# Layer 3's step reordered: maxima and copies before subtraction and exponential, counting at the end of a slot, other MLP turns, and an earlier last channel mixing

## The chip, the core and the metric

The kernel runs on one core of one Trainium2 chip. The metric is the device time of one launch in microseconds; all times below are microseconds unless they are marked ns. The core has five engines with queues of their own, each worked off in order: PE (TensorE, matrix products and transposes; its weight loads are listed as PEld), DVE (VectorE), ACT (ScalarE), POOL (GpSimd) and SP (SyncE, which here only issues DMAs). POOL issues DMAs too.

## The reference

Four layers over a batch of 4 with 512 positions and 512 channels, all in float32. Layer 0 is a cross attention with a layer norm, layers 1 and 2 are recurrent (a time mixing with a scan, then a channel mixing), and layer 3, which most of the change is in, is an attention of x over the concatenation of the context and x itself, followed by an MLP:

```python
# layers 1 and 2, the channel mixing at the end of each
xc = _ln(x, ln2_w, ln2_b)
sxc = jnp.concatenate([state[:, i0][:, None], xc[:, :-1]], axis=1) - xc
xk2 = xc + sxc * fmaa_k
xr2 = xc + sxc * fmaa_r
rr = jax.nn.sigmoid(xr2 @ fWr.T)
kk = jnp.square(jax.nn.relu(xk2 @ fWk.T))
x = x + rr * (kk @ fWv.T)
...
# layer 3: x is the context, latents are the result of layer 2
h = jnp.concatenate([x, latents], axis=1)
q = (latents @ q_w + q_b).reshape(b, k_len, NH, DH)
kv = (h @ kv_w + kv_b).reshape(b, p + k_len, NH, DH, 2)
attn = jnp.einsum('bkhd,bnhd->bhkn', q, kmat) / DH
attn = jnp.where(full_mask[:, None, None, :], attn, -jnp.inf)
attn = jax.nn.softmax(attn.astype(jnp.float32), axis=-1).astype(q.dtype)
attn_out = jnp.einsum('bhkn,bnhd->bkhd', attn, v).reshape(b, k_len, H)
attn_out = attn_out @ out_w + out_b + residual
out = rmsnorm(attn_out, postnorm_w)
out = jax.nn.gelu(out @ mlp_w1 + mlp_b1) @ mlp_w2 + mlp_b2
return out + residual
```

In layer 3 there are 16 heads of 32 channels, 512 queries and 1024 keys for each of the 4 batch entries; the mask covers the first 512 keys.

## The kernel before

The order of the instructions on PE, DVE, ACT and POOL is the order of the Python code (a manual schedule); a framework adds the semaphores and places SP's DMAs.

**The recurrent layers** work on 16 units, each of one layer, one batch entry and 256 positions. A unit takes eight scan steps g; after the last one (g = 128) the stages that follow the scan run on for some twenty steps more. `mixes`, `outputs` and `channels` are generators: each `yield g, phase` names the step, counted from the unit's first, and the place in it (EARLY, SOON, MID, LATE) where it goes on. `outputs` (steps 9 to 15) normalises the scan's result and adds it to x; for the last unit it ends at step 135. Its two powers on POOL (`gn_rs`, L932 and L934) are followed by ACT copies into `rp` and a broadcast `pbc` by PE. `channels` (steps 19 to 27) is the channel mixing: layer norm (`stats`, `scaled` into z), transposes on PE into xc (`turned`, ptn), the shifted difference sxc on POOL (`shift`), the mixtures xk and xr (`shifted`: four scalings on ACT, then `added`, an accumulating DMA that POOL issues, L583), and three products with the weights fk, fr and fv (PE tiles pm, pr, pv, all recorded under the helper line L72), of which the last is combined on DVE (L1034) and added to x by another accumulating DMA. Counted from the first unit, the last unit's channel mixing runs from step 139 to 147, the one before it from 131 to 139.

From step 129 on each step also takes one piece of layer 3's beginning (`beside`): two pieces of `begin(0)`, which transposes x of batch 0 (ptx, L1144) and adds the output bias to it on POOL (L1149), and five each of `prep(0, 0)` and `prep(0, 1)` (products pq, two pk, two pv for a group of four heads). These twelve pieces end at step 140.

**Layer 3** works through 32 units (b, m, h): batch entry, group of four heads, half of the queries (256). A unit has four steps of 256 keys, so 128 steps in all; a group (b, m) has eight, counted as c = 0 to 7 below, and a step is called a slot. The work of step i, by helper:

- `scores(i)`: 16 matmuls into the two PSUM tiles ps (L1199); they exist once, so the next step's scores need them read out.
- `kept(i, 1)` and `kept(i, 0)`: two ACT copies of ps to w in SBUF (L1213).
- `largest(i)`: four DVE instructions that keep a running maximum (L1230, L1232, L1234), with the mask for the first 512 keys.
- At a unit's end, in the first step of the next one: `gathered` transposes the maxima (ptm, L1243) and reduces them on DVE (L1244); `spread` transposes the result back (pb, L1254) and ACT copies it to mb (L1259).
- `lowered(i - 4)`: one DVE subtraction of mb from w (L1266); `weights(i - 4)`: the exponential on ACT (L1281, L1284).
- `values(i - 5)`: the products with v into po (L1305). po is one tile for both halves of the queries. In batch 0 the count of the weights (pn, by a product with ones) is accumulated by the same helper; in the other batches POOL adds the weights up (`added`, acc, L1295 and L1299), each time released by `ticked`, a tiny DVE memset and POOL copy that put it behind the subtraction (L1271, L1272), and `counted` makes pn from acc.
- `divided(unit)`: reciprocal of pn (L1332) and product with po into y (L1335).
- Turns: at the steps named in `turns` a piece of `prep` for the next group, and at those in `ready` a piece of `finish(b - 1)`, the output product (pout), the norm (its transposes ptn, L1351), and the MLP in eight blocks `hidden` (ph, Gelu L1378) and `closed` (po under L72, added to x in L1388). Each turn of `hidden` or `closed` is 32 or 16 full matmuls.

The order within a step, before: scores, one copy, counting, values (in the second step of a unit, i % 4 = 1, values come last), subtraction, the sums, exponential, maxima, the other copy, division, turns. In the first step of a unit, where mb is made, maxima and the second copy stand ahead of the subtraction. `finish` has 19 turns: two with two pout each, one with only the scaling and the transposes ptn, and two for each of eight blocks. The loop ran five slots past the last step, with the remaining turns; the last batch's `finish` came then.

## Time and profile before

| quantity | value |
|---|---|
| three runs, median | 3744.62 (3740.18 to 3747.02) |
| the profiled execution | 3743.32, span 3741.6 |
| PE busy | 3452.7, 92% of the span |
| DVE, ACT, POOL busy | 2722.9, 1904.6, 1742.6 |
| mean granted PE clock | 0.958 |
| last scan step's product (py) | at 2255.5 |
| first maxima of layer 3 (L1234) | at 2405.7 |
| groups of batch 0, start to start | 59.5, 58.9, 60.1 (the last: 64.0, first group of batch 1) |
| batches 1 to 3, from 2689.5 to the last unit's ptm | 879.1 |
| from there to the last batch's first pout | 39.4 |
| the last batch's `finish` | 133.6 |

The page tells how long each engine was busy; it cuts the span into 40 slices of some 94, lists the chain of work that ended last, and groups instructions by line with their mean length and the idle time of their engine before them. A time line of one engine gives start, length, line, operation, what it wrote and read, and in brackets the idle time before it and who ended it. A clock of 0.5 means that PE's clock was granted half of the time, and its matmuls then take about twice as long.

### The profile page before, as it was taken

The page shows a single profiled execution, that of the slowest core. Times are in us where ns is not written, and L with a number is a line of the kernel's source. Part 1 is how long each engine was busy: PE and PEld are TensorE (multiplying, and loading weights), DVE is VectorE, ACT ScalarE, POOL GpSimd, SP SyncE. Part 2 cuts the span into 40 slices and gives each one's busy share as a digit, 9 for nine tenths or more (in the row PEclk, how much of TensorE's full clock was granted, in tenths as well). Part 3 has the DMA queues.
Part 4 walks back from the last instruction along what each step waited for, and adds up shares of the span by engine and source line. Part 5 has one row for each costly group of instructions (what it writes and reads, how often), then busy time and mean ns, then how long its engine had stood idle before and what let it go on. Part 6 is the DMA issues. An engine that isn't in the chain of part 4 may idle for free. (4 is left out here: it accounts for less than half of the span.)

```text
span 3741.6 us, 55701 instructions
## 1 busy us (share of the span) xinstructions
PE 3452.7 (92%) x22400; PEld 1973.3 (53%) x22400; DVE 2722.9 (73%) x3883; ACT 1904.6 (51%) x2862; POOL 1742.6 (47%) x1040
## 2 busy tenths in 40 slices
PE   8999999998899999999999978788899999989889
PEld 3333333365566666666656634445556556555556
DVE  6777777679988888888888891287766666666631
ACT  4776776534444444444444432266555555655531
POOL 4777777524444444444444443000265555565540
PEclk9999999898999999999999988899999999999999
DMA  4000000056677777777777766100022212212124
GB/s 153 24 12 23 12 9 20 24 138 136 143 174 180 181 190 176 174 179 178 181 171 178 177 152 165 44 12 24 18 70 97 74 45 94 68 60 74 64 95 135
DMA packets 188241, 385.83 MB, mean 103 GB/s; under 512 B 18064, under 2 KB 44816, under 8 KB 185936
## 3 DMA queue, kind: packets, MB, share of 16 engines
q1 hardware_dynamic: 149680, 250.67, 20.8%
q0 software_dynamic: 38304, 131.61, 19.3%
q8 instruction: 177, 2.90, 0.3%
q14 instruction: 80, 0.66, 0.1%
HBM read 246.45 MB, written 4.19 MB: 67 GB/s over the span
## 5 line engine op out<-in xcount | busy, mean ns | idle before, releaser
L291 POOL TENSOR_TENSOR aT<-aT,nmT 128x1536 f32<-128x1536 f32 x124 | 428.8, 3462 | 206.7 <-ACT aT L289 183.4
L253 DVE CUSTOM_DVE_ANT_0 sc<-psc,nm 128x512 f32<-128x512 f32 x512 | 353.7, 691 | 147.6 <-PE psc L241 89.9
L1213 ACT COPY w<-ps 128x1024 f32<-128x1024 f32 x256 | 258.0, 1008 | 315.5 <-PE ps L1199 291.0
L870 DVE TENSOR_TENSOR ry<-kv,o_r 128x1024 f32<-128x1024 f32 x256 | 398.5, 1597 | 7.2 <-PE pm L72 0.5
L1299 POOL TENSOR_TENSOR acc<-acc,w 128x1024 f32<-128x1024 f32 x144 | 364.6, 2532 | 3.9
L1266 DVE TENSOR_TENSOR w<-w,mb 128x2048 f32<-128x2048 f32 x128 | 294.1, 2311 | 6.4 <-ACT mb L1259 6.4
L865 DVE TENSOR_TENSOR_SCAN kv<-W,kv 128x1032 f32<-128x1032 f32 x128 | 295.8, 2311 | 0.0
L289 ACT COPY aT<-pst 128x512 f32<-128x512 f32 x372 | 196.5, 594 | 179.1 <-PE pst L278 178.6
L583 POOL DMA_DIRECT2D kv<-A x127 | 111.8, 880 | 361.6 <-DVE kv L838 227.1
L1272 POOL COPY mark<-tick 128x1 f32<-128x1 f32 x118 | 63.9, 541 | 460.2 <-DVE tick L1271 376.3
L297 ACT ACTIVATE aT<-aT 128x2048 f32<-128x2048 f32 x128 | 246.7, 1929 | 5.4 <-POOL aT L291 4.7
L72 PE MATMUL po<-l_m,hT 128*128 128x512 f32 x512 | 236.1, 616 | 0.0
L72 PE MATMUL ph<-nT,l_m 128*128 128x256 f32 x1024 | 233.1, 386 | 1.4 <-DVE nT L1355 1.4
L1199 PE MATMUL ps<-q,kT 32*128 32x256 f32 x2048 | 163.7, 429 | 62.6 <-ACT w L1213 62.6
L72 PEld LDWEIGHTS ph<-nT,l_m 128*128 128x128 f32 x1024 | 195.8, 193 | 41.9 <-issue 11.6
L1230 DVE TENSOR_TENSOR run<-ps,run 128x512 f32<-128x512 f32 x256 | 170.8, 687 | 62.4 <-PE ps L1199 57.4
L278 PE MATMUL pst<-q,km 32*128 32x512 f32 x1024 | 207.1, 645 | 9.5 <-DVE mxs L253 5.8
L241 PE MATMUL psc<-km,q 32*128 32x512 f32 x1024 | 198.3, 650 | 0.8 <-ACT q L222 0.8
L884 PE MATMUL py<-ry,k 128*32 128x512 f32 x1024 | 162.5, 629 | 37.4 <-DVE ry L870 26.7
L1388 DVE TENSOR_TENSOR x<-po,x 128x512 f32<-128x512 f32 x64 | 44.1, 690 | 183.9 <-PE po L72 183.9
L832 DVE TENSOR_TENSOR kv<-vr,o_k 128x1024 f32<-128x1024 f32 x128 | 155.5, 1215 | 25.3 <-ACT S L856 25.1
L832 DVE TENSOR_TENSOR A<-vr,o_k 128x1024 f32<-128x1024 f32 x128 | 155.3, 1213 | 23.3 <-DMA kv<-A 22.9
(271 smaller groups left out, 7320.2 us busy)
## 6 DMA issues: line engine op xcount, KB each, us to landing
l_m<-in_L_W SPq DMA_DIRECT2D x64, 1024.0 KB, 5.1
kv<-A POOLq DMA_DIRECT2D x127, 516.0 KB, 6.0
L_wk<-in_L_Wk SPq DMA_DIRECT2D x16, 1024.0 KB, 7.9
L_wr<-in_L_Wr SPq DMA_DIRECT2D x16, 1024.0 KB, 7.4
L_wv<-in_L_Wv SPq DMA_DIRECT2D x16, 1024.0 KB, 5.8
L_wg<-in_L_Wg SPq DMA_DIRECT2D x16, 1024.0 KB, 8.0
L_wo<-in_L_Wo SPq DMA_DIRECT2D x64, 256.0 KB, 4.9
L_fk<-in_L_fWk SPq DMA_DIRECT2D x16, 1024.0 KB, 6.6
```

Source lines behind the costliest of these rows:

```text
L72: nc.tensor.matmul(ps, lhsT, rhs, start=(i == 0), stop=(i == len(pairs) - 1))
L241: nc.tensor.matmul(psc, d["q"][g][rs, lt * P : (lt + 1) * P], d["km"][rs, a, :], start=True, stop=True, tile_position=(32 * r, 0),)
L253: nc.vector.tensor_tensor_reduce(sc, ps[r], d["nm"][lt], 1.0, -3.0e38, ALU.add, ALU.max, mxs[:, a, lt, c : c + 1])
L278: nc.tensor.matmul(pst, d["km"][rs, a, s * P : (s + 1) * P], d["q2", a][rs, :], start=True, stop=True, tile_position=(32 * r, 0),)
L291: nc.gpsimd.tensor_tensor(w[:, n:, :], w[:, n:, :], nmT[:, None, :].to_broadcast([P, NR - n, L]), ALU.add)
L297: nc.scalar.activation(w, w, AF.Exp)
L832: nc.vector.tensor_tensor(dst[:, :, 1:], half(vrs[q, e].rearrange("p q f l -> p (q f) l")), half(d["k"][:, i : i + 1, :]).to_broadcast([P, ...
L865: nc.vector.tensor_tensor_scan(flat(kv), flat(W[g % 2]), flat(kv), 0.0, ALU.mult, ALU.add)
L870: nc.vector.tensor_tensor(y, kv[:, 4 * h : 4 * h + 4, None, :TP].to_broadcast([P, 4, 2, TP]), d["r"][:, i].rearrange("p (o m) -> p o m", o ...
L1213: nc.scalar.copy(ws[i][:, 2 * c : 2 * c + 2].rearrange("p r e q -> p (r e q)"), st[b]["ps"][c].rearrange("p r e q -> p (r e q)"),)
L1266: nc.vector.tensor_tensor(w, w, mb, ALU.subtract)
L1299: nc.gpsimd.tensor_tensor(d["acc", m, h], d["acc", m, h], w[:, :, e, :], ALU.add)
```

## The change

In the recurrent layers, the last unit's channel mixing begins three steps sooner, its xk and xr are made on DVE alone, and its last addition to x is done on DVE. Layer 3's bias adds for batch 0 are put behind the whole stage. In layer 3's step the maxima and the second copy now stand ahead of the subtraction in every step; for batches 1 to 3 the counting and the division stand behind the turns, ahead of the delayed values. The last unit's weights are counted by PE, as batch 0's are. `finish` has 18 turns; the one that held only transposes is joined to the turn before it. The turns of `prep` in the first group of batches 1 to 3 move to steps 0, 3, 4, 5 and 6. What ran past the last step is written out by hand.

The diff, without the other `yield`s that get `- sh`:

```diff
+        SHIFT = 3
...
+            ends = q == len(units) - 1
+            sh = SHIFT if ends else 0
             xs = xn[b][hf * NT : (hf + 1) * NT]
             nm, rstd = stats("cx", xs)
-            yield 21, EARLY
+            yield 21 - sh, EARLY
...
             def shifted(name, i):
                 dst = mq.tile([P, KC, TS], F32, tag="cx", name=name, bufs=BUFS["cx"])
                 for k in range(KC):
-                    nc.scalar.activation(dst[:, k], sx[:, k], AF.Copy, scale=vec[:, k, i : i + 1])
-                added(dst, cur)
+                    scale = vec[:, k, i : i + 1]
+                    if ends:
+                        nc.vector.scalar_tensor_tensor(dst[:, k], sx[:, k], scale, cur[:, k], ALU.mult, ALU.add)
+                    else:
+                        nc.scalar.activation(dst[:, k], sx[:, k], AF.Copy, scale=scale)
+                if not ends:
+                    added(dst, cur)
                 return dst
...
-            yield 27, LATE
+            yield 27 - sh, LATE
             for lt in range(NT):
-                added(xs[lt], rr[:, lt])
+                if ends:
+                    nc.vector.tensor_tensor(xs[lt], xs[lt], rr[:, lt], ALU.add)
+                else:
+                    added(xs[lt], rr[:, lt])
...
-            follow(q, (19, LATE), channels(q))
+            follow(q, (19 - (SHIFT if q == len(units) - 1 else 0), LATE), channels(q))
...
                     if k == 1:
                         yield
+                if b:
+                    biased(b)
+                yield
+
+            def biased(b):
                 for x in xn[b]:
                     nc.gpsimd.tensor_tensor(x, x, ob, ALU.add)
-                yield
...
-                if b == 0 and j == 0:
-                    d["pn"] = ps_s.tile([P, HQ], F32, tag="s", name="pn")
+                own = alone((b, m, h))
+                if own and j == 0:
+                    d["pn", m, h] = ps_s.tile([P, HQ], F32, tag="s", name="pn")
                 for e in range(2):
                     ends = dict(start=(j == 0 and e == 0), stop=(j == NS - 1 and e == 1))
                     columns(po[:, h, :], lambda r: v[:, 2 * j + e, 32 * r : 32 * r + 32], lambda r: w[:, r, e, :], **ends)
-                    if b == 0:
-                        columns(d["pn"], lambda r: ones, lambda r: w[:, r, e, :], **ends)
+                    if own:
+                        columns(d["pn", m, h], lambda r: ones, lambda r: w[:, r, e, :], **ends)
...
                 b, m, h = u
                 acc = st[b]["acc", m, h]
-                pn = st[b]["pn"] = ps_s.tile([P, HQ], F32, tag="s", name="pn")
+                pn = st[b]["pn", m, h] = ps_s.tile([P, HQ], F32, tag="s", name="pn")
...
-                    if lt % 2:
+                    if lt == 1:
                         yield
-                scaled(aos[-1], before)
                 normed(0)
                 yield
+                scaled(aos[-1], before)
...
+            def alone(u):
+                return u[0] == 0 or u == units[-1]
...
-                for c in (0, 1, 3, 5, 7) if opens or not nxt else (1, 2, 3, 5, 7) if m else (1, 2, 3, 7):
+                for c in (0, 1, 3, 5, 7) if opens or not nxt else (1, 2, 3, 5, 7) if m else (1, 2, 7):
...
-                for c in (1, 2, 4, 6, 7) if b == 0 else (2, 2, 4, 6, 6) if opens else (0, 0, 4, 6, 6):
+                at = (1, 2, 4, 6, 7) if b == 0 else (2, 2, 4, 6, 6) if opens else (0, 0, 4, 6, 6) if m else (0, 3, 4, 5, 6)
+                for c in at:
                     turns.setdefault(base + c, []).append(gen)
-            ready.update(range(NU, NU + VAL))
...
+            biased(0)
+
+            for i in range(NU):
                 over = None
-                for b0, at in ((True, i - VAL), (False, i - VAL - 1)):
-                    if 0 <= at < NU and at % NS == NS - 1 and (units[at // NS][0] == 0) == b0:
+                for own, at in ((True, i - VAL), (False, i - VAL - 1)):
+                    if at >= 0 and at % NS == NS - 1 and alone(units[at // NS]) == own:
                         over = units[at // NS]
-                last = units[i // NS - 1] if 0 < i <= NU and i % NS == 0 else None
+                last = units[i // NS - 1] if i and i % NS == 0 else None
                 low, val = i - NS, i - VAL
-                val = val if 0 <= val < NU else None
-                sums = added(val) if val is not None and units[val // NS][0] else None
+                sums = added(val) if val >= 0 and not alone(units[val // NS]) else None
                 if last:
                     gathered(last)
-                if i < NU:
-                    scores(i)
-                    kept(i, 1)
-                if over and over[0]:
-                    counted(over)
-                if val is not None and i % NS != 1:
+                scores(i)
+                kept(i, 1)
+                if val >= 0 and i % NS != 1:
                     values(val)
                 if last:
                     spread(last)
-                if sums and last:
-                    ticked()
-                    next(sums)
-                if 0 <= low < NU and not last:
+                largest(i)
+                kept(i, 0)
+                if low >= 0:
                     lowered(low)
                     if sums:
                         ticked()
                         for _ in sums:
                             pass
                     weights(low)
-                elif sums and not last:
-                    for _ in sums:
-                        pass
-                if i < NU:
-                    largest(i)
-                    kept(i, 0)
-                if last:
-                    lowered(low)
-                    if sums:
-                        ticked()
-                        for _ in sums:
-                            pass
-                    weights(low)
-                if over:
+                if over and over[0] == 0:
                     divided(over)
-                    if over[1:] == (KC - 1, 1):
-                        for _ in rest:
-                            pass
-                        rest = finish(over[0])
                 if i in ready:
                     next(rest, None)
                 for gen in turns.get(i, ()):
                     next(gen, None)
-                if val is not None and i % NS == 1:
+                if over and over[0]:
+                    counted(over)
+                    divided(over)
+                if val >= 0 and i % NS == 1:
                     values(val)
+                if over and over[1:] == (KC - 1, 1):
+                    for _ in rest:
+                        pass
+                    rest = finish(over[0])
+
+            gathered(units[-1])
+            values(NU - VAL)
+            spread(units[-1])
+            for j in range(NU - NS, NU):
+                lowered(j)
+                weights(j)
+            ticked()
+            for _ in added(NU - VAL):
+                pass
+            next(rest, None)
+            values(NU - NS)
+            values(NU - NS + 1)
+            next(rest, None)
+            values(NU - NS + 2)
+            counted(units[-2])
+            divided(units[-2])
+            values(NU - 1)
+            divided(units[-1])
             for _ in rest:
+                pass
+            for _ in finish(B - 1):
                 pass
```

`alone` and `biased` are the new functions; the rest of the calls are those described above.

More of the change, by code (lines that the diff above doesn't have):

```diff
@@ L978, in channels @@
             vec, d = small[li]["vec"], st[q]
+            ends = q == len(units) - 1
+            sh = SHIFT if ends else 0
             xs = xn[b][hf * NT : (hf + 1) * NT]
             nm, rstd = stats("cx", xs)
-            yield 21, EARLY
+            yield 21 - sh, EARLY
             z = scaled("cx", xs, nm, rstd)
-            yield 22, EARLY
+            yield 22 - sh, EARLY
             cur = mq.tile([P, KC, TS], F32, tag="xc", name="xc", bufs=1)
@@ L987, in channels @@
             nc.scalar.copy(last, cur[:, :, TS - 1])
-            yield 22, MID
+            yield 22 - sh, MID
             sx = mq.tile([P, KC, TS], F32, tag="sxc", name="sxc", bufs=1)
@@ L994, in shifted @@
                 for k in range(KC):
-                    nc.scalar.activation(dst[:, k], sx[:, k], AF.Copy, scale=vec[:, k, i : i + 1])
-                added(dst, cur)
+                    scale = vec[:, k, i : i + 1]
[5 more added lines that the diff above has]
+                    added(dst, cur)
                 return dst
-            yield 23, EARLY
+            yield 23 - sh, EARLY
             xk = shifted("xk", V_FK)
-            yield 23, LATE
+            yield 23 - sh, LATE
             xr = shifted("xr", V_FR)
-            yield 24, MID
+            yield 24 - sh, MID
             kk = mq.tile([P, KC, TS], F32, tag="cx", name="kk", bufs=BUFS["cx"])
@@ L1012, in channels @@
                 nc.scalar.activation(kk[:, m : m + 2, :], kk[:, m : m + 2, :], AF.Square, scale=0.5**0.5)
-            yield 25, MID
+            yield 25 - sh, MID
             fr = load_w(t[n + "fWr"], n + "fr")
@@ L1023, in channels @@
                 nc.scalar.activation(rr[:, lt], prs[lt], AF.Tanh, scale=0.5)
-            yield 26, MID
+            yield 26 - sh, MID
             fv = load_w(t[n + "fWv"], n + "fv")
@@ L1031, in channels @@
                 pvs.append(pv)
-            yield 27, EARLY
+            yield 27 - sh, EARLY
             for lt in range(NT):
                 nc.vector.scalar_tensor_tensor(rr[:, lt], rr[:, lt], 1.0, pvs[lt], ALU.add, ALU.mult)
-            yield 27, LATE
+            yield 27 - sh, LATE
             for lt in range(NT):
-                added(xs[lt], rr[:, lt])
+                if ends:
+                    nc.vector.tensor_tensor(xs[lt], xs[lt], rr[:, lt], ALU.add)
+                else:
+                    added(xs[lt], rr[:, lt])
         first = mixes(0)
@@ L1331, in divided @@
                 rs = sp.tile([P, C], F32, tag="rs", name="rs", bufs=1)[:, :HQ]
-                nc.vector.reciprocal(rs, d["pn"])
+                nc.vector.reciprocal(rs, d["pn", m, h])
                 if "y" not in d:
@@ L1466, in layer3 @@
             rest = iter(())
-            for i in range(NU + VAL + 1):
+            biased(0)
+            for i in range(NU):
                 over = None
-                for b0, at in ((True, i - VAL), (False, i - VAL - 1)):
-                    if 0 <= at < NU and at % NS == NS - 1 and (units[at // NS][0] == 0) == b0:
+                for own, at in ((True, i - VAL), (False, i - VAL - 1)):
+                    if at >= 0 and at % NS == NS - 1 and alone(units[at // NS]) == own:
                         over = units[at // NS]
-                last = units[i // NS - 1] if 0 < i <= NU and i % NS == 0 else None
+                last = units[i // NS - 1] if i and i % NS == 0 else None
                 low, val = i - NS, i - VAL
-                val = val if 0 <= val < NU else None
-                sums = added(val) if val is not None and units[val // NS][0] else None
+                sums = added(val) if val >= 0 and not alone(units[val // NS]) else None
                 if last:
                     gathered(last)
-                if i < NU:
-                    scores(i)
-                    kept(i, 1)
-                if over and over[0]:
-                    counted(over)
-                if val is not None and i % NS != 1:
+                scores(i)
+                kept(i, 1)
+                if val >= 0 and i % NS != 1:
                     values(val)
```

## The prediction

> **What bounds the kernel now.** I read the page's slices first, then busy time by stage, then the waits, and last the timeline of the places that the change touches. Busy time by stage (microseconds; busy time and count of each engine, granted TensorE clock, DMA):
>
> ```profile
> core 0: us, PE busy (x) PEld busy (x) DVE busy (x) ACT busy (x) POOL busy (x), PEclk, DMA share, GB/s
> 2290.30:2302.90 12.60, 0.01 (x1) 0.01 (x1) 0.00 (x0) 1.00 (x5) 11.39 (x6) 0.66 0.68 200
> 2366.50:2377.00 10.50, 0.00 (x2) 0.03 (x1) 0.00 (x0) 5.03 (x13) 3.78 (x4) 0.64 0.42 88
> 2447.00:2506.50 59.50, 50.38 (x508) 29.86 (x505) 47.95 (x51) 37.23 (x37) 0.00 (x0) 0.94 0.03 10
> 2689.50:3568.60 879.10, 810.52 (x5481) 498.82 (x5479) 575.58 (x751) 500.40 (x561) 481.83 (x295) 0.96 0.22 70
> ```
>
> The reader is to see three regimes. Between the recurrent layers and layer 3 there are two holes in which PE does nothing (rows 1 and 2). In batch 0 of layer 3 (row 3, one head group of eight steps) PE and DVE are both over 80% busy, so the order of the instructions sets the time, and not the sum of any engine. In batches 1 to 3 (row 4) PE works 92% of the time; what is lost there is PE waiting. The waits of that part (total, times, longest):
>
> ```profile
> PE pn L1305 <- POOL acc L1299: 46.8, 15, 6.0
> PE ps L1199 <- ACT w L1213: 20.6, 6, 4.4
> PE po L1305 <- DVE y L1335: 6.4, 5, 2.4
> ```
>
> pn waits for the sum on POOL, ps for the copy that stands behind the exponential. The third line is small now, but it matters most for the forecast. One of its places, in PE's timeline (start, length, idle before):
>
> ```profile
> 2985.08 1.08 PE L1305 MATMUL pn<-acc,ones 128*32 128x256 f32 x8 [3.31 <-POOL acc L1299]
> 2988.59 1.94 PE L1305 MATMUL po<-w,v 128*32 128x256 f32 x16 [2.43 <-DVE y L1335]
> ```
>
> The first values matmul of a unit waits until the unit before it has been divided, though it writes the other half of po. Where an MLP turn lies between pn and po, the division (reciprocal 1.75, product 0.42) is hidden; in this slot no turn lay there.
>
> **Part 1, between the stages.** POOL, in its order:
>
> ```profile
> 2283.16 4.95 POOL L1149 TENSOR_TENSOR x<-x,ob 128x512 f32<-128x512 f32 x4 [16.42 <-PE ptx L1144]
> 2288.07 5.45 POOL L932 TENSOR_TENSOR gn_rs<-gn_rs,mhalf 128x32 f32<-128x32 f32 x1
> 2293.50 0.69 POOL L78 TENSOR_TENSOR rs_cx<-rs_cx,mhalf 128x2 f32<-128x2 f32 x1
> 2295.69 6.11 POOL L934 TENSOR_TENSOR gn_rs<-gn_rs,mhalf 128x32 f32<-128x32 f32 x1
> ...
> 2377.00 10.19 PE L72 MATMUL pm<-xk,L_fk 128*128 128x256 f32 x32 [10.50 <-DMA xk<-xc]
> ```
>
> (1a) The bias adds (L1149) wait for ptx and hold the first power L932, whose input is ready at 2275.77 (DVE L930, 2275.54 + 0.23). Moved behind the stage, they let L932 end near 2281.2; L78 then starts when its input is there (DVE L77, 2285.76) instead of at 2293.50. From L78 to the copies of rp was 8.3 (2293.50 to 2301.83), so rp comes at 2294.1: **-7.7**. The bias itself, 4 x 1.27, runs in batch 0, where POOL is empty (row 3), and is needed first at 2689. Without that cover it would cost the 5.0.
> (1b) The last unit's channel mixing: three steps sooner its eight transposes stand ahead of two pv turns (3.7 each) instead of behind them, at 2358.3. From ptn's start to the end of the shift was 4.7 (2365.47 to 2370.2), so sx is ready at 2363.1. Four DVE multiply-adds of 0.47 (the same form, L622) replace four ACT scalings (1.70) and the accumulating DMA (2372.20 to 2377.0). They queue behind one v add (0.69): xk is there near 2365.4, and PE is free at 2366.5. fk starts 10.5 sooner: **-10.5**. The weights are no obstacle: SP issued fk, fr, fv at 2324.0, 2334.5, 2344.8, as their buffers came free. POOL's shift (2.1) now stands ahead of unit 14's two x DMAs; nobody waits for these before batch 3, but for the buffer that xr may take, 5 before pr needs it.
> (1c) fk took 10.19 after the hole, at granted clock 0.50 for its first 3.4, where the same matmuls take 7.1: **-3.1**.
> (1d) The last DMA (L1034's end 2401.71 to the first copy 2405.55, 3.8) becomes two DVE adds of 0.69: **-2.4**.
> Sum **-23.7**; bounds -14 (1c and half of 1a absent, xk late by 3) to -26 (pk, 5.7 after the first hole, back at 3.6).
>
> **Part 2, batch 0.** Pieces, start to start: four maxima 2.9 (2.7 without mask), subtraction 2.2, exponential 2.1 (1.85), a copy 0.9, scores 1.1, values with pn 1.72. I follow the queues through eight steps. After a division, the old order goes subtraction, exponential, copy, scores, values: 2.2 + 2.1 + 0.9 + 1.1 = 6.3 until the values. The new one goes maxima, subtraction, exponential: 7.2, and the values hold PE's next turn (3.4) behind them: +0.9, twice a group. At step 4 the values now wait for the exponential of step 3, behind step 3's maxima: 2.2 + 1.85 + 1.7 = 5.75 from the maxima to pb, before 3.8 (ptm, scores, values): +1.95. Together +3.85 a group; the first group has a quarter of it: **+12.5**. The same walk through the old order gives 52.4 a group where the trace has 59.5, the rest being clock and semaphores, so I trust differences only. Bounds: 0 (ps free sooner makes up for it) to +16. In batch 1's first group the spread turns give **-1.4** by the same walk.
>
> **Part 3, batches 1 to 3.** Now lost: 68 idle (72 of PE's gaps from 2663 to 3560, less 4 in batch 1's first group), and 31 because after each longer gap about 3.4 run at half clock, 1.7 each (18 gaps). pn at the end of its slot has 7 of slack over the sum, and ps is free at once: nearly all of these 99 go. In their place: pn, reciprocal, product, values with no turn between, 0.1 + 1.75 + 0.45 + 0.1 = 2.45 idle for each of 22 units, **54**. Behind the waiting values stand the next slot's scores on PE, and for these the maxima on DVE and the copies on ACT wait; both have slack there. Then the clock:
>
> ```profile
> 2577.05:2580.50 3.45, 3.45 (x5) 1.50 (x6) 3.44 (x3) 3.01 (x5) 3.45 (x2) 0.60 0.00 0
> 2643.70:2647.10 3.40, 3.08 (x48) 1.75 (x48) 3.16 (x5) 2.09 (x2) 0.00 (x0) 1.00 0.02 5
> 2648.80:2652.20 3.40, 3.40 (x36) 1.83 (x40) 2.81 (x4) 1.59 (x2) 0.00 (x0) 0.59 0.00 0
> ```
>
> The gaps before these were 1.93, 2.33 and 2.00; of six gaps from 1.9 to 2.8 four were followed by a slow stretch. So 22 x 2/3 x 1.75 = **26** (0 to 38). The Trainium skill, "TensorE: Matmul & The Clock Gate", section "HAM oscillation — how this bites in real kernels", has the rule that only idle gaps over some 3.4 us throttle the clock. By it this 26 would be nothing and the kernel about 3711; rows with 0.60 and 0.59 after gaps of 2 speak against it, so I don't use it.
> Besides: single-part slots in the first groups of batches 2 and 3, where values wait for the exponential, 3.1 each; the last group's slots without turns, 11.6 idle and two slow stretches, 15 (values wait 3.0 and scores 1.8 in each of two, 2.0 in a third); six ptm transposes whose buffer the Gelu of a hidden turn frees later, because the exponential ahead of it on ACT is later, 0.8 each. Sum 54 + 26 + 6 + 15 + 5 = 106 against 99: **+7**, bounds -20 (no slow stretch) to +23. One turn fewer removes the 4.4 wait in the slot that held only transposes (in the 99).
>
> **Part 4, the end.** From pb (3570.6) to pout 37.4 now, 30.4 without the turn that moves into the loop. New: hidden 7.1, two values with pn 3.4, a wait of 3.3 for Gelu, which ACT has behind four exponentials, closed 7.0 + 1.7 for clock, values, pn 2.2, the division 2.4, values 1.7: 28.8. **-2** (-6 to +3). The last unit's POOL sums, 19, go; pn by PE costs 4 x 0.72, in the above.
>
> **Sum.** -23.7 + 12.5 - 1.4 + 7 - 2 = -7.6. The profiled execution took 3743.3 (span 3741.6); the median of three is 3744.6, so 1.3 more. That gives **3737**.
>
> **Rivals.** (A) Slower, 0.26: the division on PE's path. What remains of the gain without it is 99 - 26 + 14.6 = 87; over 22 units it is used up at 4.0 a unit. 2.45 + 1.2 is 3.65; if the reciprocal queues behind the subtraction (L1266), as I find in single-part slots (3.9 instead of 2.45), and every gap costs 1.75, half the units come to 5.6 and half to 4.2: 108 in all, +21, 3765. For: the third wait row; against: in slots with a turn DVE has long done its subtraction. (B) Clearly faster, 0.20: the short gaps leave the clock alone, 3737 - 26 = 3711. For: 2.33 at 1.00; against: two of the three rows. (C) Much faster, 0.05: values no longer wait for y, 54 + 26 less, 3657. Against: po is one tile and the row shows the wait. (D) The moved mixing gains nothing, because xk or its buffer comes late, 0.05: -7.7 of Part 1 remains, 3753.
>
> **Chances.** My case has 0.44, its own range 3724 to 3748. 0.2% of 3744.6 is 7.5, about what a measurement can tell. It lies at that border: I give it half faster, the rest nearly all within. Faster 0.22 + 0.20 + 0.05 + a little of A and D where their price is smaller, 0.49; within 0.20; slower 0.31 with the tails of my case. Range 3702 to 3768: it leaves out C, part of B and the top of A.
>
> **What would show it.** Right: rp copies near 2294, no hole before the last fk, first run near 2382; wait rows pn <- acc nearly gone and about 22 waits po <- y of 2.4; batch-0 groups of 62 to 64 with po waiting for the exponential; a loop of batches 1 to 3 as long as now. Wrong: few po <- y waits, groups below 59 in batch 0, or the hole before fk still there.

## The result, and the profile after

The changed kernel takes 3753.25 (median of 15, 3747.09 to 3755.56), the kernel before beside it 3744.62 (median of 15). The ratio is 1.0022, with a 95% interval of 1.0014 to 1.0030: 8.2 slower, where 7.6 faster was forecast. The profiled execution has a span of 3753.9, 12.3 more than before; it is the slowest of its 15, 2.3 above their median, so the two traces differ by more than the medians do. The stages, as start to start in the two traces:

| stretch | before | after | difference | forecast |
|---|---|---|---|---|
| up to the last unit's pmean (first product of `outputs`) | 2263.45 | 2265.81 | +2.4 | 0 |
| from there to the first maxima | 142.25 | 124.56 | -17.7 | -23.7 |
| first maxima to the first group's end (ptm of step 8) | 41.3 | 44.7 | +3.4 | about +1 |
| the three other groups of batch 0 | 178.5 | 189.7 | +11.2 | about +11.5 |
| first group of batch 1 | 64.0 | 65.1 | +1.0 | -1.4 |
| from there to the last unit's ptm (below: the loop), less the turn moved in (7.0) | 878.2 | 893.1 | +14.9 | +7 |
| from there to the last pout, with that turn | 40.4 | 39.0 | -1.4 | -2 |
| last `finish` | 133.6 | 131.9 | -1.7 | 0 |

The first row is no part of the change: in the fourteen traces of this study this point lies between 2260.0 and 2266.9. The busy time by stage of the changed kernel, as shown for the one before (stretch, its length, busy time and count of PE, PEld, DVE, ACT and POOL, granted clock, DMA):

```profile
2292.63:2297.05 4.42, 0.00 (x2) 0.00 (x1) 0.00 (x0) 1.00 (x5) 3.33 (x1) 0.73 1.11 269
2361.98:2365.67 3.69, 0.00 (x1) 0.00 (x0) 3.69 (x2) 0.00 (x0) 3.35 (x3) 1.00 0.57 122
2435.10:2498.30 63.20, 51.16 (x508) 30.79 (x505) 48.77 (x50) 35.57 (x36) 0.00 (x0) 0.95 0.03 9
2689.90:3590.00 900.10, 820.84 (x5489) 500.07 (x5488) 580.61 (x730) 508.70 (x562) 414.58 (x275) 0.96 0.21 70
```

The reader is to see that the first hole shrank from 12.6 to 4.4 and the second from 10.5 to 3.7, but that this second hole, which was to close, is still there, and that DVE is busy in all of it. A group of batch 0 is 3.7 longer at nearly the same busy times. In the last row PE stands idle for 79.3 (900.10 less 820.84), before for 68.6. The waits of PE behind that row and in batch 0 (total, times, longest); first the loop:

```profile
PE po L1320 <- DVE y L1351: 59.5, 22, 4.6
PE po L1320 <- ACT w L1296: 7.1, 6, 2.9
PE ptn L1367 <- ACT ao L1445: 4.6, 3, 1.5
PE ps L1214 <- ACT w L1228: 3.0, 3, 1.6
```

The old first line, pn <- acc, is gone, and so are five sixths of ps <- w. In their place stands the division, 22 times: 17 times 2.34 or 2.43, three times 3.46 and twice 4.61. From the first maxima to the end of batch 1's first group the list had before

```profile
PE ps L1199 <- ACT w L1213: 41.9, 21, 6.3
PE po L1305 <- ACT w L1284: 3.1, 5, 2.1
```

and now it reads:

```profile
PE po L1320 <- ACT w L1299: 19.0, 15, 2.2
PE po L1320 <- ACT w L1296: 16.9, 9, 2.9
PE ps L1214 <- ACT w L1228: 15.2, 11, 3.7
```

Values wait for the exponential 24 times, 35.9 in all, as forecast; what ps gains, 26.7, is less.

### The profile page after: what moved, and what is told of

Its sections match the earlier page's. It is cut to its first block, busy times and chain, and to the rows that moved or that the text cites. A ratio compares the mean times of both kernels' runs of the same rounds, so it can differ in the third digit from the quotient of the medians.

```text
span 3753.9 us, 55692 instructions
## 1 busy us (share of the span) xinstructions
PE 3461.9 (92%) x22456; PEld 1974.8 (53%) x22456; DVE 2740.7 (73%) x3867; ACT 1905.4 (51%) x2852; POOL 1653.3 (44%) x1003
## 3 DMA queue, kind: packets, MB, share of 16 engines
q8 instruction: 178, 2.92, 0.3%
## 5 line engine op out<-in xcount | busy, mean ns | idle before, releaser
L1314 POOL TENSOR_TENSOR acc<-acc,w 128x1024 f32<-128x1024 f32 x138 | 326.5, 2366 | 5.6 <-POOL mark L1287 0.2
L1320 PE MATMUL po<-w,v 128*32 128x256 f32 x2048 | 167.4, 437 | 105.0 <-DVE y L1351 61.9
L1287 POOL COPY mark<-tick 128x1 f32<-128x1 f32 x92 | 17.0, 185 | 556.0 <-DVE tick L1286 447.2
L1299 ACT ACTIVATE w<-w,mc 128x1024 f32<-128x1024 f32 x128 | 140.0, 1141 | 132.3 <-DVE tick L1286 93.5
L1296 ACT ACTIVATE w<-w 128x2048 f32<-128x2048 f32 x64 | 122.4, 1912 | 141.4 <-DVE tick L1286 98.1
L1247 DVE SCALAR_TENSOR_TENSOR run<-ps,mc,run 128x512 f32<-128x512 f32 x192 | 143.1, 750 | 65.9 <-PE ps L1214 46.4
```

Source lines behind the costliest of these rows:

```text
L1314: nc.gpsimd.tensor_tensor(d["acc", m, h], d["acc", m, h], w[:, :, e, :], ALU.add)
L1320: nc.tensor.matmul(po[32 * r : 32 * r + 32, :], lhsT(r), rhs(r), tile_position=(0, 32 * r), **kw)
```

## The experiments

All ratios are to the kernel before, with the 95% interval, each from five rounds (4 to 11 executions); the kernel before took 3740.1 to 3740.8 beside them, so 0.001 is 3.7.

### Between the stages

The kernel before with only that part of the change. The edits are those of the diff shown, up to `biased`, and in the old loop

```diff
+            biased(0)
+
             for i in range(NU + VAL + 1):
```

> The kernel before with only the part between the stages: channel mixing three steps sooner, xk and xr on DVE, last addition on DVE, bias adds behind the stage. Theory (the new steps of layer 3 spend a real gain): layer 3 runs as before, only 17.7 us sooner, which is the difference of the two traces from pmean to the first maxima (142.25 against 124.56): about 3727, batch 0's groups at 59 to 60 and the loop of batches 1 to 3 at 878. Rival (the earlier start is given back inside layer 3, by weights or buffers that come no sooner): 3740 or more, with the first group of batch 0 longer than 41.3.

Measured: 3722.7, ratio 0.9953 (0.9940 to 0.9965), 17.6 faster. Its groups of batch 0 are 59.3, 58.8 and 57.0 (before, by the same mark, 59.5, 60.3 and 58.6), its loop 877.8. The theory holds: the gain at the seam between the stages is real, and nothing behind it gives it back. The groups show how far the same code of batch 0 differs between two traces: 3.4 in three groups.

The second run asks why the hole ahead of fk stayed. The changed kernel's timeline there (start, length, what wrote and read, idle before and who ended it):

```profile
2358.25 3.74 PE L72 MATMUL pv<-w3v,xT 128*128 128x128 f32 x32
2365.67 8.86 PE L72 MATMUL pm<-xk,L_fk 128*128 128x256 f32 x32 [3.69 <-DVE xk L1000]
...
2359.05 6.57 DVE L1000 SCALAR_TENSOR_TENSOR xk<-sxc,L_vec,xc 128x256 f32<-128x256 f32 x1
...
2359.76 5.56 POOL L1165 TENSOR_TENSOR x<-x,ob 128x512 f32<-128x512 f32 x4
```

One multiply-add of DVE takes 6.57, and it ends 0.3 after POOL's four bias adds (2365.32). The other three take 0.47 each. The adds stand behind the stage in the code, but nothing in POOL's queue holds them, so they run as soon as POOL has issued its DMAs. The edit:

```diff
-            biased(0)
-
             for i in range(NU):
...
+                if i == 12:
+                    ticked()
+                    biased(0)
                 if i in ready:
```

> The changed kernel, but the four bias adds on POOL are held back by a tick until step 12 of layer 3. Theory (the adds run beside xk on DVE and slow it: four multiply-adds took 7.75 there, and 1.66 for xr right behind them): xk takes 1.7 to 2.0, fk's products start at PE's turn, near 2362 instead of 2365.7, and without the gap they take 7.1 instead of 8.86: 5.4 less, 3748. Rival (something else makes xk slow, as the two x DMAs that POOL issues at the same time or the first run of this form): xk still takes over 6, and the time stays at 3753.

Measured: ratio 1.0011 (1.0003 to 1.0020), 4.1 less than the changed kernel. Its timeline at the same place:

```profile
2360.38 3.74 PE L72 MATMUL pv<-w3v,xT 128*128 128x128 f32 x32
2363.95 7.07 PE L72 MATMUL pm<-xk,L_fk 128*128 128x256 f32 x32
...
2361.19 1.66 DVE L1000 SCALAR_TENSOR_TENSOR xk<-sxc,L_vec,xc 128x256 f32<-128x256 f32 x4
...
2360.72 1.80 POOL L584 DMA_DIRECT2D x<-xr  x2
```

All four multiply-adds together take 1.66, and fk's products follow without a gap and at full clock. The DMA issues that the rival named still run beside xk, so they are not the cause. From pmean to the first maxima the changed kernel and the six others in which the adds run there took 123.7 to 125.6; of the six with the adds held back, five took 118.2 to 118.3 and this one 120.0.

### Batch 0

```diff
-                largest(i)
-                kept(i, 0)
+                first = i < PERIOD * KC and not last
+                if not first:
+                    largest(i)
+                    kept(i, 0)
                 if low >= 0:
                     lowered(low)
...
                     weights(low)
+                if first:
+                    largest(i)
+                    kept(i, 0)
```

> The changed kernel, but in batch 0 (the first 32 steps) subtraction and exponential stand ahead of maxima and second copy again in steps that are not the first of a unit. Theory (there the new order makes values wait for the exponential): the 24 waits po <- w (35.9 in all with batch 1's first group) nearly go, groups come back from 63.2 to 59.5 and the first from 44.7 to 41.3, together 3.4 + 3 x 3.8 = 15 less than the changed kernel, ratio to before 0.998. Rival (the groups are longer for another reason, as the joined bias adds or the clock): groups stay above 62, ratio 1.001 to 1.002.

Measured: ratio 0.9988 (0.9979 to 0.9997), so 12.7 less than the changed kernel. The first group is 41.3 again, the others 57.9, 61.7 and 57.5, and the waits of that stretch are the old ones (against 35.9 for po in the changed kernel):

```profile
PE ps L1214 <- ACT w L1228: 29.3, 20, 3.7
PE po L1320 <- ACT w L1299: 6.1, 8, 2.2
```

The order is the cause, at about the forecast price of 12.5; in the traces, batch 0 alone is 16.0 shorter than in the changed kernel.

### The place of the count and the division

Three runs. First, the changed kernel with the count early:

```diff
                 kept(i, 1)
+                if over and over[0]:
+                    counted(over)
                 if val >= 0 and i % NS != 1:
                     values(val)
...
-                if over and over[0] == 0:
+                if over:
                     divided(over)
...
-                if over and over[0]:
-                    counted(over)
-                    divided(over)
                 if val >= 0 and i % NS == 1:
```

> The changed kernel with the count of batches 1 to 3 ahead of the turns, as before, and the division ahead of them; maxima still ahead of the subtraction. Theory (count early waits for POOL's sum, and the later subtraction makes this wait longer): the 22 waits po <- y (59.5) vanish, the 14 waits pn <- acc come back at 40.8 plus up to 2.8 each, so 41 to 80; the time is 3750 to 3775. Rival (the late count alone is what made batches 1 to 3 slower, the order costs nothing): 15 less than the changed kernel, 3738.

Measured: ratio 1.0051 (1.0037 to 1.0065). pn <- acc is back with 55.4 in 20 places, longest 5.4. With the other new edits in place the late count is worth some 11; the rival falls.

Second, the count and the division in the middle of an MLP turn. `between` is called ahead of the second half of `hidden` and of `closed`, and after the second pair of pout:

```diff
+            late = []
+
+            def between():
+                if late:
+                    u = late.pop()
+                    counted(u)
+                    divided(u)
...
                     for m in range(0, KC, 2):
+                        if m:
+                            between()
                         pm = ps_s.tile([P, 2, T2], F32, tag="s", name="ph")
...
+                if over and over[0]:
+                    late.append(over)
+                    if i not in ready:
+                        between()
                 if i in ready:
                     next(rest, None)
                 for gen in turns.get(i, ()):
                     next(gen, None)
-                if over and over[0]:
-                    counted(over)
-                    divided(over)
+                between()
```

> The changed kernel with the count and the division in the middle of an MLP turn instead of behind it: half of the turn's matmuls (3.6), pn, the other half, then the values; where a slot holds only a piece of prep, the count is ahead of it. Theory (the price of batches 1 to 3 is the division on PE's path, and the clock after it): the waits po <- y fall from 59.5 to under 8, pn <- acc to under 10, and of 15 slow clock windows (37.5 lost) about 10 go, 17 us; the loop falls from 900 to 825 to 840 and the time to about 3680. Rival (another engine or the order of maxima sets the pace there): the waits move to pn <- acc, ph or ps, the loop stays above 880, the time above 3733.

Measured: 3705.56, ratio 0.9911 (0.9897 to 0.9924): 41.5 less than the changed kernel and 33 less than the one before. The waits of its loop:

```profile
PE po L1320 <- DVE y L1351: 11.9, 13, 2.5
PE pn L1320 <- POOL acc L1314: 9.5, 5, 3.7
PE po L1320 <- ACT w L1296: 8.2, 6, 2.9
```

The loop is 853.4 against 900.1. po <- y fell by 47.6, and PE's time at half clock costs 16.1 instead of 32.7 (half of PE's busy time in the stretches with granted clock 0.50; the expectation had 37.5). The kind is as the theory says, the size two thirds of it: pn and po are not quite free of waits, and PE's busy time less that half-clock loss rose from 788 to 793.5. About half of that rise is in ph's products (2.8), whose turns are cut in two; that the halves overlap less is likely, but no run shows it.

Third, the late count alone, on the kernel of the first experiment, with the old order, turns and end:

```diff
-                if over and over[0]:
+                hands = over and over[1:] == (KC - 1, 1)
+                late = over and over[0] and not hands
+                if over and over[0] and hands:
                     counted(over)
...
                 for gen in turns.get(i, ()):
                     next(gen, None)
+                if late:
+                    counted(over)
+                    divided(over)
                 if val is not None and i % NS == 1:
```

> The kernel before with the part between the stages (as in the first experiment, 3722.7) and only the count and the division of batches 1 to 3 behind the turns; order of the step, turns and end are the old ones, and the count at the handover between batches stays early. Theory (the late count trades one wait for another that is as long or longer): pn <- acc falls from 40.8 to about 10, po <- y comes to 20 x 2.34 = 47, the clock loses as much as before; loop 878 to 890 or 895, time about 3738, ratio 0.9995. Rival (the late count is a gain and what costs is the order or the turns): loop under 872, ratio under 0.994.

Measured: 3728.2, ratio 0.9962 (0.9950 to 0.9975), loop 881.5, against 0.9953 and 877.8 without it. The waits of the loop:

```profile
PE po L1320 <- DVE y L1350: 54.9, 22, 3.4
PE ps L1214 <- ACT w L1228: 10.6, 6, 2.9
PE pn L1320 <- POOL acc L1314: 6.6, 2, 3.3
```

In the same stretch of the kernel before:

```profile
PE pn L1305 <- POOL acc L1299: 40.8, 14, 4.9
```

One wait is traded for another: pn <- acc 40.8 becomes 6.6, po <- y 6.4 becomes 54.9. The sum comes to less than I expected, because ps <- w was halved too. A difference of 0.0009 lies within the two intervals. The late count was worth some 11 with the other new edits in place (the first run above); with the old ones no gain shows.

### The order and the turns of batches 1 to 3

The run above, with maxima and second copy ahead of the subtraction from step 32 on:

```diff
-                if 0 <= low < NU and not last:
+                first = last or PERIOD * KC <= i < NU
+                if 0 <= low < NU and not first:
                     lowered(low)
...
                     kept(i, 0)
-                if last:
+                if first:
                     lowered(low)
```

> The one above, and maxima and second copy ahead of the subtraction from batch 1 on (turns and end still the old ones). Theory: the waits ps <- w (20.6) go, as with the count in the middle of a turn, where this order was worth 15.6 in the loop and cost 7.5 in batch 1's first group: 8 less than the run above, 3730; the changed kernel with batch 0 in the old order (0.9988) is then 6 slower than this, which is the price of its turns and its end. Rival (the turns and the end are a gain): this is slower than 0.9988.

Measured: 3767.4, ratio 1.0067 (1.0054 to 1.0080): 39 slower than the run above, where 8 faster was expected. The theory falls and its rival holds: the changed kernel with batch 0 in the old order is at 0.9988, so the new turns and the new end, with the other differences between these two kernels (the count at the handover of a batch, the last unit counted by PE), are a gain of 29.5. The waits of the loop show what the order does:

```profile
PE po L1320 <- DVE y L1350: 56.8, 20, 5.5
PE po L1320 <- ACT w L1296: 13.9, 5, 2.9
PE po L1320 <- ACT w L1299: 12.8, 2, 6.4
```

26.7 of waits of values for the exponential are new. They arise as in batch 0, where PE has no turn between one step's scores and the values: twice 6.40 in slot 5 of the first groups of batches 2 and 3, three times 2.92 behind the turn that holds only transposes, the rest in the last group. The new turns put a piece of `prep` into that slot 5 and join the transposes to another turn. The account closes: in the loop idle time rose from 72.9 to 98.3, half clock from 29.9 to 36.7 and PE's own work by 2.3, and batch 1's first group from 64.1 to 68.6, together 39.0.

The same question with the division out of the way: the kernel that joins all three edits so far (below), with the old order in all batches (`first = not last`).

> As the kernel with the three edits together, but with subtraction and exponential ahead of maxima and second copy in all batches. Theory (the order costs nothing and brings nothing in batches 1 to 3, where PE has MLP turns to do): the loop of batches 1 to 3 within 8 of that kernel's. Rival (the order is what frees ps early there): over 15 longer, by waits ps <- w.

Measured: 3692.7, ratio 0.9874 (0.9860 to 0.9888), against 0.9839 with the new order from batch 1 on. The loop is 15.6 longer, batch 1's first group 7.5 shorter. So here the new order is a gain, as the rival said, but little of it is ps <- w (10.3 against 4.7): pn <- acc is 34.7 in 13 places instead of 9.1 in 3. One of them, in PE's, DVE's and POOL's timeline:

```profile
2717.76 0.64 PE L1320 MATMUL pn<-acc,ones 128*32 128x256 f32 x8 [2.12 <-POOL acc L1314]
...
2708.39 4.49 DVE L1281 TENSOR_TENSOR w<-w,mb 128x2048 f32<-128x2048 f32 x2
...
2710.76 2.17 POOL L1287 COPY mark<-tick 128x1 f32<-128x1 f32 x1 [7.91 <-DVE tick L1286]
2712.89 4.82 POOL L1314 TENSOR_TENSOR acc<-acc,w 128x1024 f32<-128x1024 f32 x2
```

In the old order the subtractions of a unit's first two steps stand back to back on DVE. POOL's tiny copy, released after the first, takes 2.17 (it does so 19 times in this trace) instead of 0.18, and ends with the second; both adds come some 2 late. The kernel before had one of the two adds earlier for this place (`if sums and last`), which the change dropped. So this run doesn't have the whole old order, and what the old order with its early add would cost with the new turns stays open.

And the order on the kernel with old turns and the count in the middle of a turn, from step 40 on (the same edit, `PERIOD * (KC + 1)`):

> The fastest so far (old turns, old end, count in the middle of a turn, ratio 0.9808) with maxima and second copy ahead of the subtraction from batch 1's second group on. Theory (that order frees ps early where PE has MLP turns): the waits ps <- w (11.6) go, loop from 829.7 to 815 to 825, ratio 0.977 to 0.980. Rival (it makes POOL's sum later, and the count in the middle of a turn then waits for it): pn <- acc over 25, ratio over 0.981.

Measured: 3713.3, ratio 0.9927 (0.9915 to 0.9939), where that kernel without the order has 0.9808: 44 slower. The rival is right about the direction and wrong about the reason: pn <- acc is only 2.8, while po <- w grew from 3.9 to 31.3 and po <- y from 15.1 to 27.2.

### Versions that beat both

All three edits on the changed kernel (bias adds at step 12, old order in batch 0, count in the middle of a turn):

> The three edits together on the changed kernel: bias adds held back to step 12, old order in batch 0, count and division in the middle of a turn. Theory (the three prices lie in different stages and add up): 0.9911 - (1.0022 - 1.0011) - 15/3740 = 0.986 of the kernel before, about 3688 where before is 3740. Rival (they share a wait, so that one hides another's gain): over 3700.

Measured: 3681.15, ratio 0.9839 (0.9825 to 0.9852). The prices add up and a little more (0.986 was the sum).

The kernel before with the new seam (the part between the stages), the adds at step 12 and the count in the middle of a turn, everything else old. `between` is as above, and the count at the handover of a batch stays early:

```diff
+                hands = over and over[1:] == (KC - 1, 1)
-                if over and over[0]:
+                if hands and over[0]:
                     counted(over)
+                if over and over[0] and not hands:
+                    late.append(over)
...
-                if over:
+                if over and (hands or over[0] == 0):
                     divided(over)
```

> The kernel before with the part between the stages (bias adds at step 12) and the count and division in the middle of an MLP turn, but its own order of the step, its own turns and its own end. Only the count at the handover from one batch to the next stays early. Theory (in batches 1 to 3 only the place of the count and the division matters, the new order and turns bring little): the loop falls from 878 to 815 to 840, with 6 waits ps <- w of 20 left, and the time to 3740 - 17.6 - 4.3 - 50 = 3668. Rival (the count can only move because the new order and turns make room): waits pn <- acc stay above 25, the loop above 850, the time above 3690.

Measured: 3669.5, ratio 0.9808 (0.9792 to 0.9824), the fastest here: 71 less than the kernel before beside it (3740.8). Its loop by stage, and its waits:

```profile
2665.00:3494.70 829.70, 794.34 (x5474) 488.93 (x5473) 580.50 (x750) 499.94 (x559) 479.19 (x295) 0.98 0.23 75
...
PE po L1320 <- DVE y L1350: 15.1, 5, 3.4
PE pn L1320 <- POOL acc L1314: 13.9, 4, 6.0
PE ps L1214 <- ACT w L1228: 11.6, 6, 2.9
```

PE is busy for 96% of the loop, against 92% before. The theory holds to a microsecond and a half (3668), and its rival falls: neither the new order nor the new turns were needed to move the count.

The kernel with three edits, old order also in batch 1's first group (`PERIOD * (KC + 1)`), and `between` one product earlier in the slot of pout:

```diff
                 for lt in range(LT):
+                    if lt == 3:
+                        between()
                     pm = ps_s.tile([P, C], F32, tag="s", name="pout")
...
-                between()
                 normed(0)
```

> The kernel with the three edits together, old order kept through batch 1's first group as well, and in the slot that holds pout the count one product earlier. Theory: first group of batch 1 back from 66.3 to 58.8, and three waits po <- y of 2.46 with the clock after them less, 4: 3681 - 7.5 - 4 = 3670, ratio 0.981. Rival (batch 1's second group takes the time back): over 3678.

Measured: 3675.2, ratio 0.9823 (0.9810 to 0.9836); batch 1's first group is 58.8. The gain of 0.0016 is half of what was expected, and the interval doesn't tell it from the kernel with all three edits.

### The change in single steps

Four of these runs and the changed kernel form a chain from the kernel before to the changed one, each with one part more. In microseconds of 3740, from the ratios:

| part | ratio after it | price |
|---|---|---|
| between the stages | 0.9953 | -17.6 |
| count and division late in batches 1 to 3 | 0.9962 | +3.4 |
| maxima and copies first in batches 1 to 3 | 1.0067 | +39.3 |
| turns, end, last unit counted by PE, late count at the handover of a batch too, no early add | 0.9988 | -29.5 |
| maxima and copies first in batch 0 | 1.0022 | +12.7 |

Each ratio is uncertain by some 0.001, so each price by about 6. The prices belong to this sequence; the order of batches 1 to 3 and the turns are not independent.

## Why the prediction was wrong

**Part 1** failed where (1a) meets (1b). (1a) says that the bias "runs in batch 0, where POOL is empty", at no cost, and (1b), that "xk is there near 2365.4", by four multiply-adds of 0.47. From the transposes ptn to a complete xk this reckons 7.1. The adds ran at 2359.76 instead, beside xk, and it took 13.0 (2353.80 to 2366.80); with the adds held back it is 6.9. So the place of the adds was wrong, and the wait of DVE for POOL was put at nothing. Moving them in the code moved them past `outputs`, but POOL reached them before the stage was over. Most runs with the adds held back show 118.3 from pmean to the first maxima (the one that differs from the changed kernel by nothing else, 120.0), those without some 124; 118.3 is 23.9 less than before, the forecast's -23.7. So (1a), (1c) and (1d) were right in kind and in sum (pbc came 8.2 sooner for 7.7; fk's start to the first maxima went from 28.7 to 24.7, and to 22.9 with the adds held back, for a forecast of 23.2), and the miss of 6 is this one step.

The answer from which the 0.47 was read could have warned of it. It is the median of the same form (shortest, median and longest in ns) in the kernel before:

```profile
L622 DVE SCALAR_TENSOR_TENSOR mixx<-sx,L_vec,xa x60: 468/472/2567, 773.0 to 2090.1; 128x256 f32<-128x256 f32 x60
L622 DVE SCALAR_TENSOR_TENSOR sx<-sx,L_vec,xa x4: 471/560/3653, 637.1 to 641.6; 128x256 f32<-128x256 f32 x4
```

The two longest, 3.65 at 637.66 and 2.57 at 773.02, each ran beside one POOL operation (3.61 from 637.42, 2.38 from 772.93) and ended 0.3 after it.

**Part 2** was right in kind and nearly in size: +12.5 forecast (its pieces add up to 3.75 a group, where it has 3.85), 12.7 by the run that undoes it and 14.6 by the two traces, with the waits that were named. Batch 1's first group, -1.4, came out at +1.0; the runs that keep the old order there (58.8 against 66.3 with the count in mid-turn) show that the new order costs something in that group too, which the walk missed.

**Part 3** was right in its mechanism, and the sum of its terms was too small; this is the other step that failed. The old loss was reckoned at 99 and is 99.6 (68.6 idle, and 31.0 of half clock while PE was busy). The new loss was 106 and is 112.0: idle 79.3 for 76.6, half clock 32.7 for 29.4. The division itself is 59.5 for 54: seventeen waits are of the forecast length, but in three slots the reciprocal queues behind the norm's work on DVE (3.46), and in two, single-part slots, behind the subtraction and an addition to v (4.61). Half clock followed 8 of the 17 short waits, where two thirds were reckoned, and all five long ones, which cost 2.7 to 2.9 each instead of 1.7: 27.4 together, so that the forecast 26 came out near by luck. PE's busy time less the half-clock loss rose by 2.5 besides the moved turn, for which there was no term; it is spread over ptn (0.9) and several other products, and why it rose stays open. Together 2.7 + 3.3 + 2.5 - 0.6 = 7.9, so +14.9 for +7.

What Part 3 did not see is that its +7 is a small difference of large prices. It put the new cost down to the division. The single steps show the late count nearly neutral (+3.4), the new order of the step at +39 by itself, and the new turns and end at -29.5, where they fill slots in which that order hurts.

**Part 4**, -2, came out at -1.4, and the last `finish` was 1.7 shorter without a term for it.

**The rivals.** (A) had the right sign. Its price for the division was too high in most slots: the reciprocal was held up in 5 places of 22, not in half of them; in two of the five its reason, the queue behind the subtraction, was the right one. That the division on PE's path was the largest single loss that remained is shown by the run with the count in mid-turn, 41.5 less. (B) and (C) fell: half clock followed short gaps, and values did wait for y. (D) named 3753, which is what was measured, but that is luck: xk did come late, but Part 1 still gained 17.7, where (D) left 7.7, and the loop cost 7.9 more than (D) had it. The forecast stood 7.6 from no change with two terms of 6 to 8 off in the same direction, and that turned its sign.

## What to carry to other kernels

When a change moves an operation off one path, look where the operation lands: an instruction placed later in the code runs as early as its own queue lets it, and what runs beside it then is part of its price. A small serial chain (product, reciprocal, product) costs its length wherever PE has nothing between its two ends; splitting a long stretch of PE work and putting the chain in the middle paid 41.5 here, while moving the count from one end to the other paid some 11 with the new order and nothing that could be told with the old. The order within a step and the spread of other work over the steps are one decision, and taken one at a time they gave +39 and -29.5, where the forecast had one +7 for all of batches 1 to 3.

## What the runs showed of the hardware

**The clock is granted in fixed windows.** All stretches at half clock in a trace start on a grid of 3.413. Two waits of the same 2.34 in the changed kernel, by windows of that grid (columns as above; the clock is the third number from the end):

```profile
2755.46:2758.87 3.41, 1.14 (x20) 0.56 (x24) 2.18 (x2) 3.38 (x6) 2.38 (x1) 1.00 0.82 258
2758.87:2762.28 3.41, 3.41 (x32) 1.62 (x32) 1.50 (x3) 1.20 (x3) 0.00 (x0) 0.50 0.13 50
...
2796.42:2799.83 3.41, 2.15 (x16) 1.21 (x14) 1.19 (x1) 3.38 (x4) 1.05 (x1) 1.00 0.11 29
2799.83:2803.24 3.41, 2.33 (x38) 1.31 (x42) 1.14 (x3) 1.40 (x5) 1.30 (x1) 1.00 0.77 278
2803.24:2806.65 3.41, 3.41 (x22) 1.50 (x15) 3.34 (x5) 3.09 (x3) 0.00 (x0) 1.00 0.00 0
```

The first wait lies in one window, PE is busy for 1.14 of 3.41, and the next window is at half clock. The second is cut by a window's edge, PE is busy for 2.15 and 2.33, and the clock stays. Counted over layer 3 (windows from 2400 to the last matmul) in all fourteen traces: after full-rate windows in which PE was busy for less than 45%, 281 of 282 were followed by half clock; at 45 to 55%, 33 of 126; above 55%, 3 of 4508. From half clock, all 134 windows under 75% busy were followed by another, and none of 321 from 85% on. This is no complete rule: ahead of 2400, nearly all of it in the other layers, half clock followed 91 of 8866 full-rate windows above 55%, and 98 of 371 half-clock windows from 85% on, and no run here shows why. For layer 3, the forecast's "two thirds" is close to the chance that a gap of 2.34 puts more than half a window into one window, (3.41 - 2.34 + 2 x 0.63) / 3.41 = 0.68, and by this count, as an estimate, gaps under some 1.7 cost little clock there when they stand alone. The Trainium skill, "TensorE: Matmul & The Clock Gate", section "HAM oscillation — how this bites in real kernels", has only gaps longer than some 3.4 throttle. The window's length agrees with the grid measured here, the condition doesn't: in layer 3 about half a window idle was enough.

**POOL and DVE hold each other up.** A DVE multiply-add with two inputs in SBUF took 6.57 beside four POOL adds, and 0.47 without them; a POOL copy took 2.17 beside a DVE subtraction, and 0.18 without. The Trainium skill, "SBUF — State Buffer", section "SBUF: two separate sides", says that such a pair shares a port as an exclusive lock, held by whichever starts first for its whole instruction. The rows agree that one holds up the other, with one thing more: DVE waited not for one add (1.9) but until the fourth had ended, though its own instruction is listed as started 0.7 before the first.
